# Graph layers on one core: products with adj as seven block products over pairs of batches, and one PSUM pool of eight banks

## The chip, the core and the metric

The kernel runs on one core of a Trainium2 chip. The metric is the device time of one execution in microseconds (us). The kernel before was run three times: median 1768.22 us, 1768.13 to 1768.93. One further execution was taken with the hardware profiler: 1770.05 us, of which 1768.3 us lie between its first and last instruction (the span).

Engines are named as in the profile: PE is the matrix engine (TensorE), PEld its weight loads, DVE the vector engine, ACT the scalar engine, POOL GpSimd, SP the engine that issues most transfers. PSUM is the memory that matmuls write to; the kernel uses it as eight banks of 128 x 512 f32 each. DVE and ACT read and write it.

## What is computed

x has 32 batches of 512 nodes by 128 channels, adj is 512 x 512, all in f32. Layer 0 is a graph convolution with three powers of adj, layer 1 five steps of a gated recurrent unit whose inputs are products with adj. Both get a residual and a layer norm. Cut to what matters:

```python
# layer 0: both "adjacencies" are adj, so the weights of equal powers add up
p1 = adj @ x; p2 = adj @ p1; p3 = adj @ p2
y  = x @ W[0] + p1 @ (W[1] + W[4]) + p2 @ (W[2] + W[5]) + p3 @ (W[3] + W[6])
h0 = layernorm(x + y)
# layer 1: 5 times, from h = h0; av = [m, m]
m  = adj @ h
u  = h @ u3.T + u3_b
z  = sigmoid([m, m] @ w3.T + w3_b + u)
r  = sigmoid([m, m] @ w4.T + w4_b + u)
hv = tanh([m, m] @ w5.T + w5_b + (r * h) @ u5.T + u5_b)
h  = (1 - z) * h + z * hv
out = layernorm(h0 + h)
```

## The kernel before

The host lays out adj transposed (adjT). The 32 batches go in eight groups of four (GB = 4). A batch is held twice: as nodes by channels, four tiles of 128 x 128 (xg, h0, h), and transposed, 128 channels by 512 nodes (xT, hT). The halves of w3, w4 and w5 are added once at the start (L103 to L108), so that one 128 x 128 weight serves.

**Layer 0** (L156 to L222) takes for each batch four transposes (ptr_x, L142), the product with adj (pt, L166: four matmuls of 512 columns, summed in one bank), a copy by ACT (tT), and eight matmuls of 128 columns into pq (L180, L181), which DVE copies to U. For the four batches together py (L190 to L202) applies adj squared (at2, made once) to U and adds the rest. ACT copies it to v, DVE takes moments, POOL the power -0.5 (rstd, L127), DVE normalises to h0 (L136), and four transposes per batch give the first hT.

**Layer 1** (L224 to L276) runs over five steps and in each over the group's four batches. I call one batch in one step a batch-step; there are 8 x 5 x 4 = 160. On PE it is:

- the product with adj: pm, four matmuls of 512 columns (L233), copied by ACT to mT (L237);
- pu (L239), then pr (L244), pz (L251) and w5, the first matmul into ph (L257), one matmul each;
- u5, the second matmul into ph (L258), which needs rh. rh comes from pr by a DVE addition (L245), ACT's sigmoid (L246) and a DVE product (L248). DVE's addition for pz (L252) stands between;
- four transposes into ptr_h (L142), which need the new hT. It comes from ph by ACT's tanh (L259) and three DVE operations (L261, L262, L264). ACT copies them back to h (L270), the operand of the next step's pm.

In the last step DVE adds h0 instead (L272) and last_norm follows (L145 to L154): moments, rstd on POOL, four normalisations (y), and a store by SP.

**What sets the order.** Each engine executes its own queue in order. The framework's scheduler makes the queues from the written order, the dependencies and its own model of time. It also hands out the buffers of the pools: here four pools of two PSUM banks (ps_mm, ps_zr, ps_hv, ps_tr). Layer 0 of the next group is a generator. After each batch-step but the group's first, the main loop (L282 to L288) lets it write one further piece, so that layer 0 of group g + 1 is written in between layer 1 of group g. On PE's queue of the old program the order is not the written one: the product of the next batch is placed between w5 and u5 of this one, and between u5 and the transposes.

Of the kernel before, what the change touches and what calls it, by code (L numbers as in the profile page):

```python
# [8 lines left out]
F32 = mybir.dt.float32  # L9
AF = mybir.ActivationFunctionType  # L10
ALU = mybir.AluOpType
PSUM = bass.MemoryType.PSUM

P = 128
NK = 4
# [7 lines left out]
def gnn_resnorm_kernel(  # L23
# [24 lines left out]
    small = ctx.enter_context(tc.tile_pool(name="small", bufs=4))  # L48
    ps_mm = ctx.enter_context(tc.tile_pool(name="ps_mm", bufs=2, space=PSUM))
    ps_zr = ctx.enter_context(tc.tile_pool(name="ps_zr", bufs=2, space=PSUM))  # L50
    ps_hv = ctx.enter_context(tc.tile_pool(name="ps_hv", bufs=2, space=PSUM))
    ps_tr = ctx.enter_context(tc.tile_pool(name="ps_tr", bufs=2, space=PSUM))

    def load_x(g):
        xg = grp.tile([P, NK, GB, P], F32, tag="xg", name=f"xg_{g}")
        for b in range(GB):
            nc.sync.dma_start(
                xg[:, :, b, :], x[g * GB + b].rearrange("(p k) c -> p k c", k=NK)
            )
        return xg  # L60
# [21 lines left out]

    an = const.tile([P, NK, N], F32, tag="an", name="an")
    at2 = const.tile([P, NK, N], F32, tag="at2", name="at2")
    for km in range(NK):
        ptr = ps_tr.tile([P, NK, P], F32, tag="tr", name=f"ptr_a_{km}")
        for k in range(NK):
            nc.tensor.transpose(ptr[:, k, :], at[:, k, km * P : (km + 1) * P], ident)
        nc.scalar.copy(an[:, km, :], ptr.rearrange("p k c -> p (k c)"))
    for k in range(NK):  # L90
        pq = ps_mm.tile([P, N], F32, tag="mm", name=f"pq_{k}")
        for km in range(NK):
            nc.tensor.matmul(  # L93
                pq,
                lhsT=an[:, km, k * P : (k + 1) * P],
                rhs=at[:, km, :],
                start=(km == 0),
                stop=(km == NK - 1),
            )
        nc.vector.tensor_copy(at2[:, k, :], pq)  # L100


# [35 lines left out]
    def transposed(src_of, name):  # L138

        ptr = ps_tr.tile([P, NK, P], F32, tag="tr", name=f"ptr_{name}")  # L140
        for k in range(NK):
            nc.tensor.transpose(ptr[:, k, :], src_of(k), ident)  # L142
        return ptr

    def last_norm(g, b, h):  # L145
# [10 lines left out]
    def layer0(g, xg, done):  # L156

        xTs, tTs = [], []
        U = grp.tile([P, NK, GB, P], F32, tag="U", name=f"U_{g}")
        for b in range(GB):  # L160
            ptr = transposed(lambda k: xg[:, k, b, :], f"x_{g}_{b}")
            xT = work.tile([P, NK, P], F32, tag="xT", name=f"xT_{g}_{b}", bufs=5)
            nc.scalar.copy(xT, ptr)
            pt = ps_mm.tile([P, NK, P], F32, tag="mm", name=f"pt_{g}_{b}")
            for k in range(NK):
                nc.tensor.matmul(  # L166
                    pt.rearrange("p k n -> p (k n)"),
                    lhsT=xg[:, k, b, :],
                    rhs=at[:, k, :],
                    start=(k == 0),  # L170
                    stop=(k == NK - 1),
                )
            tT = work.tile([P, NK, P], F32, tag="tT", name=f"tT_{g}_{b}", bufs=5)
            nc.scalar.copy(tT, pt)
            xTs.append(xT)
            tTs.append(tT)
            yield
            pq = ps_mm.tile([P, NK, P], F32, tag="mm", name=f"pq_{g}_{b}")
            for k in range(NK):
                nc.tensor.matmul(pq[:, k, :], lhsT=xT[:, k, :], rhs=wc[:, 2, :], start=True, stop=False)  # L180
                nc.tensor.matmul(pq[:, k, :], lhsT=tT[:, k, :], rhs=wc[:, 3, :], start=False, stop=True)  # L181
            nc.vector.tensor_copy(U[:, :, b, :], pq)  # L182
            yield

        v = grp.tile([P, NK, GB * P], F32, tag="v", name=f"v_{g}")
        mv = small.tile([P, NK * GB, 2], F32, tag="mv0", name=f"mv0_{g}")
        for ko in range(NK):
            py = ps_mm.tile([P, GB * P], F32, tag="mm", name=f"py_{g}_{ko}")
            for k in range(NK):
                nc.tensor.matmul(  # L190
                    py,
                    lhsT=at2[:, k, ko * P : (ko + 1) * P],
                    rhs=U[:, k, :, :].rearrange("p b o -> p (b o)"),
                    start=(k == 0),
                    stop=False,
                )
            for b in range(GB):
                dst = py[:, b * P : (b + 1) * P]
                nc.tensor.matmul(dst, lhsT=xTs[b][:, ko, :], rhs=wc[:, 0, :], start=False, stop=False)  # L199
                nc.tensor.matmul(  # L200
                    dst, lhsT=tTs[b][:, ko, :], rhs=wc[:, 1, :], start=False, stop=(b == GB - 1)
                )  # L202
            nc.scalar.copy(v[:, ko, :], py)
            for b in range(GB):
                moments(mv[:, ko * GB + b, :], v[:, ko, b * P : (b + 1) * P], f"{g}_{ko}_{b}")
            yield

        h0 = grp.tile([P, NK, GB, P], F32, tag="h0", name=f"h0_{g}")
        rstd = rstd_of(mv, NK * GB, f"0_{g}")
        hT = []  # L210
        for b in range(GB):
            for k in range(NK):
                i = k * GB + b
                normalise(
                    h0[:, k, b, :], v[:, k, b * P : (b + 1) * P], mv[:, i, 0:1], rstd[:, i : i + 1]
                )
            ptr = transposed(lambda k: h0[:, k, b, :], f"h0_{g}_{b}")
            t = work.tile([P, NK * P], F32, tag="hT0", name=f"hT_{g}_{b}_init", bufs=6)
            nc.scalar.copy(t, ptr.rearrange("p k c -> p (k c)"))
            hT.append(t)  # L220
            yield
        done.append((h0, hT))  # L222

    def layer1(g, h0, hT):  # L224


        h = [h0[:, :, b, :] for b in range(GB)]
        for s in range(STEPS):
            for b in range(GB):
                nm = f"{g}_{s}_{b}"  # L230
                pm = ps_mm.tile([P, N], F32, tag="mm", name=f"pm_{nm}")
                for k in range(NK):
                    nc.tensor.matmul(  # L233
                        pm, lhsT=h[b][:, k, :], rhs=at[:, k, :], start=(k == 0), stop=(k == NK - 1)
                    )
                mT = work.tile([P, N], F32, tag="mT", name=f"mT_{nm}")
                nc.scalar.copy(mT, pm)  # L237
                pu = ps_mm.tile([P, N], F32, tag="mm", name=f"pu_{nm}")
                nc.tensor.matmul(pu, lhsT=u3s, rhs=hT[b], start=True, stop=True)  # L239
                uT = work.tile([P, N], F32, tag="uT", name=f"uT_{nm}")  # L240
                nc.scalar.activation(uT, pu, AF.Identity, bias=ub3s)  # L241

                pr = ps_zr.tile([P, N], F32, tag="zr", name=f"pr_{nm}")
                nc.tensor.matmul(pr, lhsT=w4s, rhs=mT, start=True, stop=True)  # L244
                nc.vector.scalar_tensor_tensor(pr, pr, b4s, uT, ALU.add, ALU.add)  # L245
                nc.scalar.activation(pr, pr, AF.Sigmoid)  # L246
                rh = work.tile([P, N], F32, tag="rh", name=f"rh_{nm}")
                nc.vector.tensor_tensor(rh, pr, hT[b], ALU.mult)  # L248

                pz = ps_zr.tile([P, N], F32, tag="zr", name=f"pz_{nm}")  # L250
                nc.tensor.matmul(pz, lhsT=w3s, rhs=mT, start=True, stop=True)  # L251
# [3 lines left out]

                ph = ps_hv.tile([P, N], F32, tag="hv", name=f"ph_{nm}")
                nc.tensor.matmul(ph, lhsT=w5s, rhs=mT, start=True, stop=False)  # L257
# [4 lines left out]
                nc.vector.tensor_tensor(ph, ph, z, ALU.mult)  # L262
                hT_new = work.tile([P, NK * P], F32, tag="hT", name=f"hT_{nm}", bufs=8)
                nc.vector.tensor_tensor(hT_new, ph, hT[b], ALU.add)  # L264
                hT[b] = hT_new

                ptr = transposed(lambda k: hT_new[:, k * P : (k + 1) * P], f"h_{nm}")
                h_new = work.tile([P, NK, P], F32, tag="h", name=f"h_{nm}", bufs=6)
                if s < STEPS - 1:
                    nc.scalar.copy(h_new, ptr)  # L270
                else:
                    nc.vector.tensor_tensor(h_new, ptr, h0[:, :, b, :], ALU.add)  # L272
                h[b] = h_new
                if s == STEPS - 1:
                    last_norm(g, b, h_new)
                yield  # L276
# [5 lines left out]
    for g in range(NG):  # L282
        ahead = layer0(g + 1, load_x(g + 1), done) if g + 1 < NG else iter(())
        for i, _ in enumerate(layer1(g, *done[g])):
            if i >= 1:
                next(ahead, None)
# [55 lines left out]
```

## Time and profile before

| | |
|---|---|
| median of three runs | 1768.22 us (1768.13 to 1768.93) |
| the profiled execution | 1770.05 us |
| its span | 1768.3 us, 14169 instructions |
| mean granted clock of PE | 0.991 |
| a group's share, from 488 to 700 us | 212 us, PE busy 209.59, DVE 104.70, ACT 77.77, POOL 6.92 |
| read from and written to memory | 10.42 and 8.39 MB |
| a 512-column f32 matmul | two records of 592 ns, each at least 0.43 us after the one before |
| a load of x for one batch | 256 KB, 4.4 us to landing |

A matmul in f32 shows as two records with a weight load each, a transpose as one. Records of matmuls overlap: the next starts while one drains, so spacing and duration differ. Busy time counts overlapping records once. "Idle" in brackets is the time in which the engine did nothing ahead of an instruction, with what it waited for. The granted clock is the share of PE's full clock that the hardware allowed in a stretch.

### The profile page before, as it was taken

Reading aid. Unit: us, or ns where it says so; the run is one execution under the profiler, and the core shown is the slowest. Engines: PE = TensorE matmul, PEld = TensorE weight load, DVE = VectorE, ACT = ScalarE, POOL = GpSimd, SP = SyncE. Lnnn points to the kernel's source line nnn. Section 1 sums busy time; section 2 is a strip of 40 time slices with the busy share of each in tenths; the row PEclk is TensorE's granted clock in tenths of the full one; section 3 lists DMA queues with packets and bytes.
Section 4 is the critical chain, followed back from the end, with each engine's and each line's share of the span. In section 5 each row is a group of like instructions: output and inputs, shape, how many; then the busy total and the mean of one; then the engine's idle time right before and its main releaser. Section 6 shows DMA issues by size and latency. Waiting matters only on the chain.

```text
span 1768.3 us, 14169 instructions
## 1 busy us (share of the span) xinstructions
PE 1717.5 (97%) x5360; PEld 845.7 (48%) x5360; DVE 856.6 (48%) x1845; ACT 640.6 (36%) x1062; POOL 56.1 (3%) x46
## 2 busy tenths in 40 slices
PE   6899999999999999999999999999999999999997
PEld 3545544455445554455544555445544455444443
DVE  1244347444574445744356444564445543466556
ACT  1143334333433333333343332433324333344442
POOL 0000000000000000000000000000000000000000
PEclk9999999999999999999999999999999999999998
DMA  3000000000000000000000000000000000000000
GB/s 94 24 1 0 24 1 18 6 24 0 1 24 0 24 1 0 24 0 24 1 0 24 0 24 1 6 19 0 0 1 12 12 0 1 1 13 12 1 0 24
DMA packets 23684, 19.72 MB, mean 11 GB/s; under 512 B 1856, under 2 KB 19264, under 8 KB 23488
## 3 DMA queue, kind: packets, MB, share of 16 engines
q1 hardware_dynamic: 21504, 16.78, 3.0%
q10 hardware_dynamic: 2112, 2.03, 0.4%
q8 instruction: 42, 0.69, 0.2%
q14 instruction: 26, 0.21, 0.0%
HBM read 10.42 MB, written 8.39 MB: 11 GB/s over the span
## 4 chain that ended last, share of the span: by engine, by line
PE 93%; DVE 4%; POOL 1%; DMA 1%; issue 0%; ACT 0%; POOLq 0%; SPq 0%; DVEq 0%
PE pm L233 29%; PE ph L258 8%; PE pr L244 8%; PE pz L251 7%; PE pu L239 7%; PE ph L257 7%; PE py L190 6%; PE pt L166 6%; PE ptr_h L142 5%; PE pq L181 2%; PE py L200 2%; PE py L199 2%; PE pq L180 2%; POOL rstd L127 1%; DVE h L136 1%; PE pq L93 1%
## 5 line engine op out<-in xcount | busy, mean ns | idle before, releaser
L233 PE MATMUL pm<-at,h 128*128 128x512 f32 x1280 | 599.8, 598 | 0.0
L233 PEld LDWEIGHTS pm<-at,h 128*128 128x128 f32 x1280 | 239.6, 193 | 269.0 <-issue 269.0
L245 DVE SCALAR_TENSOR_TENSOR pr<-pr,b4s,uT 128x512 f32<-128x512 f32 x160 | 121.2, 757 | 418.7 <-PE pr L244 410.5
L237 ACT COPY mT<-pm 128x512 f32<-128x512 f32 x160 | 93.6, 585 | 353.8 <-PE pm L233 353.8
L261 DVE TENSOR_TENSOR ph<-ph,hT 128x512 f32<-128x512 f32 x128 | 89.4, 699 | 205.7 <-ACT ph L259 205.7
L259 ACT ACTIVATE ph<-ph,hv_b 128x512 f32<-128x512 f32 x160 | 105.9, 662 | 220.4 <-PE ph L258 220.4
L258 PE MATMUL ph<-rh,u5s 128*128 128x512 f32 x320 | 170.1, 614 | 16.1 <-DVE rh L248 16.1
L244 PE MATMUL pr<-mT,w4s 128*128 128x512 f32 x320 | 171.4, 617 | 0.0
L251 PE MATMUL pz<-mT,w3s 128*128 128x512 f32 x320 | 163.5, 592 | 0.0
L257 PE MATMUL ph<-mT,w5s 128*128 128x512 f32 x320 | 163.4, 592 | 0.0
L246 ACT ACTIVATE pr<-pr 128x512 f32<-128x512 f32 x160 | 93.4, 584 | 180.8 <-DVE pr L245 180.7
L239 PE MATMUL pu<-hT,u3s 128*128 128x512 f32 x256 | 130.8, 592 | 0.0
L252 DVE SCALAR_TENSOR_TENSOR pz<-pz,b3s,uT 128x512 f32<-128x512 f32 x160 | 121.0, 757 | 17.0 <-PE pz L251 13.5
L241 ACT ACTIVATE uT<-pu,ub3s 128x512 f32<-128x512 f32 x160 | 109.9, 687 | 42.4 <-PE pu L239 42.4
L190 PE MATMUL py<-U,at 128*128 128x512 f32 x256 | 119.7, 592 | 0.8 <-DVE U L182 0.8
L166 PE MATMUL pt<-at,xg 128*128 128x512 f32 x256 | 119.7, 592 | 0.0
L270 ACT COPY h<-ptr_h 128x512 f32<-128x512 f32 x128 | 74.9, 585 | 116.1 <-PE ptr_h L142 116.1
L142 PEld LDWEIGHTS ptr_h<-ident,hT 128*128 128x128 f32 x640 | 77.4, 141 | 82.2 <-issue 39.0
L254 ACT ACTIVATE z<-pz 128x512 f32<-128x512 f32 x160 | 95.5, 597 | 53.1 <-DVE pz L252 51.9
L262 DVE TENSOR_TENSOR ph<-ph,z 128x512 f32<-128x512 f32 x160 | 111.6, 698 | 4.5
L127 POOL TENSOR_TENSOR rstd<-ve,mhalf 128x4 f32<-128x4 f32 (+1 forms) x40 | 55.4, 1385 | 1707.3 <-DVE ve L125 1707.3
L142 PE MATMUL ptr_h<-ident,hT 128*128 128x128 f32 x640 | 97.1, 274 | 6.2 <-DVE hT L264 4.1
(59 smaller groups left out, 1420.7 us busy)
## 6 DMA issues: line engine op xcount, KB each, us to landing
xg<-in_x SPq DMA_DIRECT2D x32, 256.0 KB, 4.4
out<-y SPq DMA_DIRECT2D x32, 256.0 KB, 2.0
at<-in_adjT ACTq DMA_DIRECT2D x1, 1024.0 KB, 6.5
w_raw<-in_w ACTq DMA_DIRECT2D x1, 448.0 KB, 3.2
w3s_raw<-in_w ACTq DMA_DIRECT2D x1, 128.0 KB, 6.0
w4s_raw<-in_w ACTq DMA_DIRECT2D x1, 128.0 KB, 5.4
w5s_raw<-in_w ACTq DMA_DIRECT2D x1, 128.0 KB, 5.4
u3s<-in_u ACTq DMA_DIRECT2D x1, 64.0 KB, 4.6
```

The source lines that it names most:

```text
L142: nc.tensor.transpose(ptr[:, k, :], src_of(k), ident)
L166: nc.tensor.matmul(pt.rearrange("p k n -> p (k n)"), lhsT=xg[:, k, b, :], rhs=at[:, k, :], start=(k == 0), stop=(k == NK - 1),)
L190: nc.tensor.matmul(py, lhsT=at2[:, k, ko * P : (ko + 1) * P], rhs=U[:, k, :, :].rearrange("p b o -> p (b o)"), start=(k == 0), stop=False,)
L233: nc.tensor.matmul(pm, lhsT=h[b][:, k, :], rhs=at[:, k, :], start=(k == 0), stop=(k == NK - 1))
L239: nc.tensor.matmul(pu, lhsT=u3s, rhs=hT[b], start=True, stop=True)
L244: nc.tensor.matmul(pr, lhsT=w4s, rhs=mT, start=True, stop=True)
L245: nc.vector.scalar_tensor_tensor(pr, pr, b4s, uT, ALU.add, ALU.add)
L251: nc.tensor.matmul(pz, lhsT=w3s, rhs=mT, start=True, stop=True)
L252: nc.vector.scalar_tensor_tensor(pz, pz, b3s, uT, ALU.add, ALU.add)
L257: nc.tensor.matmul(ph, lhsT=w5s, rhs=mT, start=True, stop=False)
L258: nc.tensor.matmul(ph, lhsT=u5s, rhs=rh, start=False, stop=True)
L262: nc.vector.tensor_tensor(ph, ph, z, ALU.mult)
```

## The change

Three things change.

**Products with adj over pairs of batches.** With node blocks of 256 and two batches side by side, the operand and adj's transpose are each 2 x 2 blocks, and their product needs eight block products the plain way. The new `adj_product` takes seven (Winograd's form). Four sums T of adj's blocks are made once by DVE (new L109 to L113). Four sums S of the batches' blocks are made each time by POOL, 128 x 256 each (L162 to L165). Each block product is two matmuls of 256 columns. Three banks collect them: pb one product; pc two; pa four one after another, and ACT copies pa out after each, three times to Q and at last to m1, while the sum goes on. DVE adds pb and pc to copies in Q (three additions). The results m0 and m1 take the place of tT in layer 0 and mT in layer 1, for two batches.

```diff
+    def adj_product(X, name):
+        X11, X12, X21, X22 = X[:, 0, :H], X[:, 0, H:], X[:, 1, :H], X[:, 1, H:]
+        S = work.tile([P, 4, H, P], F32, tag="S", name=f"S_{name}", bufs=3)
+        nc.gpsimd.tensor_tensor(S[:, 0], X21, X22, ALU.add)
+        nc.gpsimd.tensor_tensor(S[:, 1], S[:, 0], X11, ALU.subtract)
+        nc.gpsimd.tensor_tensor(S[:, 2], X11, X21, ALU.subtract)
+        nc.gpsimd.tensor_tensor(S[:, 3], X12, S[:, 1], ALU.subtract)
...
+        pa, pb, pc = (bank(f"p{i}_{name}")[:, :HN] for i in "abc")
...
+        product(pa, X11, B11, True, False)
+        nc.scalar.copy(Q[:, 0], pa)
+        product(pb, X12, B21, True, True)
+        product(pa, S[:, 1], T[:, 1], False, False)
+        nc.vector.tensor_tensor(m0[:, :HN], pb, Q[:, 0], ALU.add)
+        nc.scalar.copy(Q[:, 1], pa)
+        product(pc, S[:, 0], T[:, 0], True, False)
+        product(pa, S[:, 2], T[:, 2], False, False)
+        nc.scalar.copy(Q[:, 2], pa)
+        nc.vector.tensor_tensor(m1[:, HN:], pc, Q[:, 2], ALU.add)
+        product(pa, X22, T[:, 3], False, True)
+        nc.scalar.copy(m1[:, :HN], pa)
+        product(pc, S[:, 3], B22, False, True)
+        nc.vector.tensor_tensor(m0[:, HN:], pc, Q[:, 1], ALU.add)
+        return m0, m1
```

**One PSUM pool.** Every PSUM tile is now one of eight banks of a single pool.

```diff
-    ps_mm = ctx.enter_context(tc.tile_pool(name="ps_mm", bufs=2, space=PSUM))
-    ps_zr = ctx.enter_context(tc.tile_pool(name="ps_zr", bufs=2, space=PSUM))
-    ps_hv = ctx.enter_context(tc.tile_pool(name="ps_hv", bufs=2, space=PSUM))
-    ps_tr = ctx.enter_context(tc.tile_pool(name="ps_tr", bufs=2, space=PSUM))
+    psum = ctx.enter_context(tc.tile_pool(name="psum", bufs=8, space=PSUM))
+
+    def bank(name):
+        return psum.tile([P, N], F32, tag="bank", name=name)
```

**Where the pieces are cut.** The product is written ahead of each pair's first batch, with a yield behind it, in both layers. Layer 0's transposes of x come behind the product. The main loop lets layer 0 go on after every second piece of layer 1, and after all of them from the 21st on.

```diff
-                pm = ps_mm.tile([P, N], F32, tag="mm", name=f"pm_{nm}")
-                for k in range(NK):
-                    nc.tensor.matmul(
-                        pm, lhsT=h[b][:, k, :], rhs=at[:, k, :], start=(k == 0), stop=(k == NK - 1)
-                    )
-                mT = work.tile([P, N], F32, tag="mT", name=f"mT_{nm}")
-                nc.scalar.copy(mT, pm)
+                if b % 2 == 0:
+                    m = adj_product(h[b // 2], f"h_{nm}")
+                    if s < STEPS - 1:
+                        h[b // 2] = work.tile([P, 2, NK, P], F32, tag="h", name=f"h_{nm}", bufs=4)
+                    yield
+                mT = m[b % 2]
...
         for i, _ in enumerate(layer1(g, *done[g])):
-            if i >= 1:
+            if i % 2 == 1 or i > 20:
                 next(ahead, None)
```

Besides, xg and h0 are stored batch by batch, h holds two batches per tile, U has one buffer instead of two, and some buffer counts change (uT and rh 3, h 4, mT 6).

## The prediction

> **What bounds the kernel now.** The first view is the page's busy times, with the shares of the chain that ended last:
>
> ```profile
> PE 1717.5 (97%) x5360; PEld 845.7 (48%) x5360; DVE 856.6 (48%) x1845; ACT 640.6 (36%) x1062; POOL 56.1 (3%) x46
> ...
> PE 93%; DVE 4%; POOL 1%; DMA 1%; issue 0%; ACT 0%; POOLq 0%; SPq 0%; DVEq 0%
> ```
>
> TensorE (PE) is full: it idles 1768.3 - 1717.5 = 51 us in all, two thirds of that before the loop and in its last 20 us. So both the matmul work and anything that opens a hole in PE's in-order queue count in full. How it is kept full is seen in the timeline of one batch-step (start, duration, engine, line):
>
> ```profile
> 700.18 1.02 PE L244 MATMUL pr<-mT,w4s 128*128 128x512 f32 x2
> 701.04 1.02 PE L251 MATMUL pz<-mT,w3s 128*128 128x512 f32 x2
> 701.31 0.76 DVE L245 SCALAR_TENSOR_TENSOR pr<-pr,b4s,uT 128x512 f32<-128x512 f32 x1 [2.38 <-PE pr L244]
> 701.90 1.02 PE L257 MATMUL ph<-mT,w5s 128*128 128x512 f32 x2
> ...
> 702.10 0.58 ACT L246 ACTIVATE pr<-pr 128x512 f32<-128x512 f32 x1 [0.95 <-DVE pr L245]
> ...
> 702.76 1.02 PE L233 MATMUL pm<-at,h 128*128 128x512 f32 x2
> ...
> 702.77 0.68 DVE L248 TENSOR_TENSOR rh<-pr,hT 128x512 f32<-128x512 f32 x1
> ...
> 703.61 1.02 PE L258 MATMUL ph<-rh,u5s 128*128 128x512 f32 x2
> ...
> 704.47 2.74 PE L233 MATMUL pm<-at,h 128*128 128x512 f32 x6
> ...
> 704.67 0.66 ACT L259 ACTIVATE ph<-ph,hv_b 128x512 f32<-128x512 f32 x1 [1.19 <-PE ph L258]
> ...
> 705.37 0.70 DVE L261 TENSOR_TENSOR ph<-ph,hT 128x512 f32<-128x512 f32 x1 [1.92 <-ACT ph L259]
> ...
> 706.10 0.70 DVE L262 TENSOR_TENSOR ph<-ph,z 128x512 f32<-128x512 f32 x1
> ...
> 706.83 0.69 DVE L264 TENSOR_TENSOR hT<-ph,hT 128x512 f32<-128x512 f32 x1
> ...
> 707.05 1.02 PE L239 MATMUL pu<-hT,u3s 128*128 128x512 f32 x2
> ...
> 707.91 0.60 PE L142 MATMUL ptr_h<-ident,hT 128*128 128x128 f32 x4
> ```
>
> Two chains leave PE and come back. From pr (700.18) through DVE, ACT and DVE, rh is ready at 702.77 + 0.68 = 703.45, and 0.06 later (as where PE really waits, below) u5, the second matmul into ph, could start: 3.33 after pr. From u5 (703.61) through tanh and three DVE operations hT is ready at 707.52; with the 0.15 between hT and the transposes seen at the end of the trace they could start 4.06 after u5. PE fills both times with the next batch's product with adj: one matmul of pm before u5, three and pu after it. In the order of the old program's instructions at least 0.86 us of such other work stands before u5 in 159 of the 160 batch-steps, and at least 3.43 us between u5 and the transposes, also in 159. The last batch has no other work, and there the trace shows the bare price (idle time in brackets; its 3.63 has 0.6 of DVE's y in it):
>
> ```profile
> 1759.55 1.09 PE L142 MATMUL ptr_h<-ident,hT 128*128 128x128 f32 x4 [3.63 <-DVE hT L264]
> ```
>
> Third, what a hole does to the clock. Stretches of 3.41 us: PE busy is the second number, the granted clock (PEclk) the one before the DMA share:
>
> ```profile
> 461.80:465.20 3.40, 1.62 (x4) 0.87 (x5) 2.23 (x6) 1.64 (x3) 0.00 (x0) 1.00 0.00 0
> 465.20:468.60 3.40, 3.40 (x12) 1.55 (x11) 2.36 (x4) 1.48 (x3) 0.00 (x0) 1.00 0.00 0
> ```
> ```profile
> 673.41:676.82 3.41, 1.33 (x5) 0.27 (x3) 3.41 (x10) 1.18 (x2) 0.00 (x0) 1.00 0.00 0
> 676.82:680.23 3.41, 3.41 (x4) 1.48 (x5) 1.06 (x3) 0.66 (x1) 0.00 (x0) 0.50 0.03 5
> ```
>
> Once per group u5 waits 2.08 us. In five groups of seven the idle time lies in one clock window, which is 39% busy, and the next window runs at 0.50; in the other two (47% here) nothing happens. In all of them pm stands ready behind u5 and isn't run first: PE does not pass a waiting matmul.
>
> **The matmul work.** A 512-column f32 matmul is two records, 0.43 us start to start, 0.86 together; a 128-column one takes 0.223 (layer 0: six in 1.34). On that line 256 columns cost 0.435 (between half of 0.86 and twice 0.223). A pair of batches had 8 x 0.86 = 6.88; it gets 14 x 0.435 = 6.09. There are 80 pairs in layer 1 and 16 in layer 0: 96 x 0.79 = **-76 us**.
>
> **The lost cover.** This is what decides. In the order of the new program pr, pz, w5, u5 and the four transposes stand directly one after another in all 160 batch-steps. The products and layer 0's pieces come behind the transposes, or ahead of pr. So u5 waits 3.33 - 3 x 0.86 = 0.75 us, and the transposes 4.06 - 0.86 = 3.20, with the next pu or product queued behind them. For 159 batch-steps: 119 + 509 = **+628 us**.
>
> **Waits inside the product.** In 45 of 80 pairs pr follows the last product directly and waits for m0: matmul drain 0.16 (a record of 592 ns at a spacing of 429), 0.11 to DVE, its 256-column add, 0.06 back. An add of 256 isn't in the trace: between 0.29 (128 columns, L107) and 0.70 (512, L261); on the line between, 0.43. That is 0.76 x 45 = +34 (28 to 46). The third use of pa waits for ACT's copy of 256 columns, between 0.29 (half of 0.585) and 0.585; I take the middle, 0.44. It is hidden by 0.87 of other products or pu, except in 30 pairs where only four transposes (0.44) stand between: 0.26 x 30 = +8 (3 to 12). In 14 pieces of layer 0 xT's copy stands behind h's on ACT, and the transposes cover 0.87 of 1.9: +14. Each new semaphore wait on PE may hold back the weight load ahead, between 0 and 0.08 (pr to pz is 0.94 instead of 0.86 where pr has just waited): about 5 in each of 96 products, middle 0.04, +19 (0 to 38). In return the old 0.08 at pr goes, -13. The normalisation of h0 still stands in DVE's queue ahead of a chain once per group, now with two more operations inside it: +4.
>
> **What costs nothing.** The copies and adds are 4 x 0.44 on ACT and 3 x 0.43 on DVE per pair, less two copies of 0.585; with PE at over 25 us per pair neither is near full. If they were late, they would be late at the waits priced above. POOL's four sums work on h finished a pair earlier, over 15 us. No 256-column sum is in the trace: a 128-column select on POOL took 0.29; rstd's power, 16 columns, 2.90, which at that rate would be 46 us. By kind an add is nearest to the select; 0.6 to 1.2 each, 5 us a pair at most. Only from about 4 us each does PE wait. rstd now stands behind up to four sums; its readers (y) are off the path. The x loads land in 4.4 us, a group ahead.
>
> **The clock.** Holes of about 3.0 us (3.20 less the drain), after one of 0.6, come 160 times. Halving takes 1.8 to 2.1 us idle in a 3.41 us window; with 1.95 the window may start anywhere in 3.15 us around the hole: 92%. The half-speed window then begins 1.35 to 4.5 us after the hole's start; on average 2.96 us of it lie behind the hole and cost half, 1.48: 160 x 0.92 x 1.48 = 218. If a half-speed window that is partly idle doesn't release the clock, about 290; some falls on pz and w5, which have room. I take **+240** (100 to 400). The 8.5 of the old five windows go.
>
> The Trainium skill, "TensorE: Matmul & The Clock Gate" (Part 1: The HAM clock gate), has the clock fall only after a whole idle window of about 3.4 us. By it these holes would cost no clock and the sum would be 2380. The 39% window above says otherwise, and I follow it.
>
> **Sum**, against the profiled execution: 1768.3 - 76 + 628 + 34 + 8 + 14 + 19 - 13 + 4 - 8 + 240 = 2618; with 1.75 around the span, as there (1770.05), **2620 us**. The shown median, 1768.22, is 0.1% below the profiled run, far less than any term.
>
> **Rivals.**
> - The waits come, the clock stays up: 2620 - 240 = 2380. For it: two of seven holes didn't drop it. Against: 3 us is half as long again. 0.10.
> - Faster: PE does not stand at the transposes, since the queued product runs past the waiting matmul, and the two chains stay covered as now. Then only the -76 and the small waits (34 + 8 + 14 + 19 - 13 + 4 = 66) are left: 1760; without those, 1694. It decides once 618 of the 628 us are covered. Against it: u5's 2.08 us with pm ready behind. 0.03.
> - A new engine bounds: POOL's sums, above 4 us each. At 8 us a pair takes 32 us, 96 pairs 3070 us. For it only the power's rate. 0.03.
> - The clock hardly recovers, since each half-speed window holds the next hole: two windows per hole, 160 x 2 x 1.7 = 544, 2920. Against: a fully busy window releases it, and between holes lie 5 to 12 us of work. 0.06.
>
> The forecast's own case, clock cost 100 to 400, has 0.78. The range 2400 to 2800 reaches to the first rival's edge and takes in the other bounds (together about 60 us either way). Slower by over 0.2% (about what a measurement of this kernel can tell from no change): 0.965; within it 0.005; faster 0.03.
>
> **What would show it.** PE's busy share near 72% (68 to 76); PE's waits led by the transposes for hT, about 500 us in 160 times, then u5 for rh, about 120; 256-column records 0.217 apart; mean granted clock about 0.90 instead of 0.99 (160 x 0.92 windows of 3.41 us at half); POOL's sums under 1.2 us. Wrong it would be if the transposes' wait is under 1 us each, if the clock stays at 0.99 (2380), or if the 256-column records are bound by their 0.19 us weight loads plus a wait each and come 0.3 apart (+220).

## The result and the profile after

The changed kernel takes 2688.76 us (median of four runs, 2688.23 to 2689.09), the kernel before took 1768.58 us beside it. The ratio is 1.52, with a 95% interval of 1.517 to 1.523: half as long again. The forecast was 2620 us.

The busy times and the shares of the chain that ended last, of the changed kernel:

```profile
PE 2028.6 (75%) x6512; PEld 1249.5 (46%) x6512; DVE 997.5 (37%) x2137; ACT 683.1 (25%) x1254; POOL 326.4 (12%) x430
...
PE 69%; DVE 23%; ACT 4%; issue 2%; POOL 1%; DMA 0%; ACTq 0%; POOLq 0%; DVEq 0%
```

Two things are to be seen. PE is no longer full: it idles 2687.3 - 2028.6 = 659 us instead of 51, and DVE's share of the chain has gone from 4% to 23%. And PE is busy 311 us longer than before, although the products got smaller. Busy time that grows while the work shrinks is for the most part work done at a lower clock. (A smaller part is how it is counted: the last 0.16 us of a matmul, which the next one used to cover, now count by themselves ahead of each of the 365 waits in the first three lines below, some 58 us.)

PE's waits name the idle time (line waited for: us in total, times, longest):

```profile
PE ptr_h L155 <- DVE hT L309: 502.6, 160, 5.1
PE ph L303 <- DVE rh L293: 95.0, 160, 0.9
PE pr L289 <- DVE m_h L196: 23.2, 45, 0.5
PE pq L225 <- ACT xT L220: 10.8, 16, 0.7
```

The first two lines hold 598 of the 659 us, once in each of the 160 batch-steps. No line names POOL. The timeline of one batch-step shows them in place:

```profile
1004.93 1.02 PE L289 MATMUL pr<-m_h,w4s 128*128 128x512 f32 x2
1005.79 1.02 PE L296 MATMUL pz<-m_h,w3s 128*128 128x512 f32 x2
1006.65 1.02 PE L302 MATMUL ph<-m_h,w5s 128*128 128x512 f32 x2
...
1007.52 0.68 DVE L293 TENSOR_TENSOR rh<-pr,hT 128x512 f32<-128x512 f32 x1
1008.25 1.13 PE L303 MATMUL ph<-rh,u5s 128*128 128x512 f32 x2 [0.58 <-DVE rh L293]
...
1011.64 0.69 DVE L309 TENSOR_TENSOR hT<-ph,hT 128x512 f32<-128x512 f32 x1
1012.38 1.12 PE L155 MATMUL ptr_h<-ident,hT 128*128 128x128 f32 x4 [3.00 <-DVE hT L309]
...
1014.14 1.84 PE L284 MATMUL pu<-hT,u3s 128*128 128x512 f32 x2
```

u5 starts 3.32 us after pr and the transposes 4.13 us after u5, as long as the chains through DVE and ACT take; nothing lies inside but this batch's own pz and w5. And the pu behind them takes 1.84 us instead of 1.02. The stretches of 3.41 us around it say why (PE busy is the second number, the granted clock the one before the DMA share):

```profile
1005.53:1008.95 3.42, 2.84 (x7) 0.89 (x6) 2.11 (x3) 1.47 (x3) 0.00 (x0) 1.00 0.00 0
1008.95:1012.36 3.41, 0.43 (x1) 0.00 (x0) 2.09 (x3) 0.66 (x1) 0.00 (x0) 1.00 0.00 0
1012.36:1015.78 3.42, 3.40 (x10) 2.44 (x11) 0.00 (x0) 1.17 (x2) 0.00 (x0) 0.50 0.02 5
...
1036.26:1039.67 3.41, 1.13 (x2) 0.30 (x2) 1.40 (x3) 0.87 (x2) 0.00 (x0) 1.00 0.00 0
1039.67:1043.08 3.41, 2.47 (x6) 1.59 (x7) 2.13 (x7) 0.00 (x0) 0.00 (x0) 0.50 0.00 0
1043.08:1046.50 3.42, 3.42 (x5) 1.35 (x4) 1.33 (x6) 1.15 (x2) 0.00 (x0) 0.50 0.00 0
1046.50:1049.91 3.41, 2.22 (x5) 0.49 (x3) 2.53 (x7) 1.16 (x3) 1.02 (x1) 1.00 0.00 0
```

A stretch that is 13% busy (0.43 of 3.41) is followed by one at 0.50, and that one, full, by one at 1.00. The second hole costs two: the half-speed stretch itself is only 72% busy (2.47), and the next one is still at 0.50. A stretch at full speed that is 65% busy (2.22) has done no harm. Over the whole trace the clock falls 162 times and lies at half for 774 us, which is 227 such stretches. PE is busy for 657 us of them; half of that, 329 us, is time that full speed would have saved, if half the clock makes all of it twice as long.

### The profile page after: what moved, and what is told of

The parts are those of the page before. It is cut to its first block, busy times and chain, and to the rows that moved or that the text cites. A ratio compares the mean times of both kernels' runs of the same rounds, so it can differ in the third digit from the quotient of the medians.

```text
span 2687.3 us, 17885 instructions
## 1 busy us (share of the span) xinstructions
PE 2028.6 (75%) x6512; PEld 1249.5 (46%) x6512; DVE 997.5 (37%) x2137; ACT 683.1 (25%) x1254; POOL 326.4 (12%) x430
## 4 chain that ended last, share of the span: by engine, by line
PE 69%; DVE 23%; ACT 4%; issue 2%; POOL 1%; DMA 0%; ACTq 0%; POOLq 0%; DVEq 0%
PE pa_h L174 13%; PE pu L284 6%; PE ph L303 6%; PE pr L289 6%; PE ptr_h L155 6%; PE py L236 6%; PE pc_h L174 5%; PE pz L296 5%; DVE ph L307 4%; DVE ph L306 4%; DVE hT L309 4%; DVE pz L297 4%; ACT ph L304 4%; PE pb_h L174 4%; DVE rh L293 4%; PE pa_x L174 3%
## 5 line engine op out<-in xcount | busy, mean ns | idle before, releaser
L155 PE MATMUL ptr_h<-ident,hT 128*128 128x128 f32 x640 | 153.7, 386 | 502.6 <-DVE hT L309 502.6
L162 POOL TENSOR_TENSOR S_h<-h 128x256 f32<-128x256 f32 x80 | 57.8, 723 | 1725.5 <-ACT h L314 1699.9
L289 PE MATMUL pr<-m_h,w4s 128*128 128x512 f32 x320 | 199.5, 710 | 23.2 <-DVE m_h L196 23.2
L296 PE MATMUL pz<-m_h,w3s 128*128 128x512 f32 x320 | 176.9, 636 | 0.0
L174 PE MATMUL pa_h<-T,S_h 128*128 128x256 f32 x640 | 169.3, 388 | 0.0
L302 PE MATMUL ph<-m_h,w5s 128*128 128x512 f32 x320 | 163.4, 592 | 0.0
L303 PEld LDWEIGHTS ph<-rh,u5s 128*128 128x128 f32 x320 | 47.6, 188 | 227.5 <-DVE rh L293 227.5
L174 PE MATMUL pa_h<-at,h 128*128 128x256 f32 x320 | 142.0, 594 | 0.0
L174 PEld LDWEIGHTS pa_h<-T,S_h 128*128 128x128 f32 x640 | 127.4, 199 | 20.8
L289 PEld LDWEIGHTS pr<-m_h,w4s 128*128 128x128 f32 x320 | 71.2, 234 | 118.8 <-issue 69.9
```

The lines of the kernel that those rows point to most:

```text
L155: nc.tensor.transpose(ptr[:, k * P : (k + 1) * P], src_of(k), ident)
L174: nc.tensor.matmul(dst, lhsT=left[:, k, :], rhs=right[:, k, :], start=(first and k == 0), stop=(last and k == H - 1), skip_group_check=True,)
L303: nc.tensor.matmul(ph, lhsT=u5s, rhs=rh, start=False, stop=True)
```

## Experiments

The theory that the experiments test has two parts. One ring of eight banks for all PSUM tiles makes the scheduler keep the written order, so that nothing stands between a batch's own matmuls; and the holes that this opens halve the clock. The rivals: the seven-product form itself (POOL's sums, more waits, shorter matmuls) brings the loss; or the clock is of no account, and the idle time and some other delay explain it all. Each run is given with the kernel before beside it; ratios have a 95% interval.

### One ring of banks in the kernel before

```diff
-    ps_mm = ctx.enter_context(tc.tile_pool(name="ps_mm", bufs=2, space=PSUM))
-    ps_zr = ctx.enter_context(tc.tile_pool(name="ps_zr", bufs=2, space=PSUM))
-    ps_hv = ctx.enter_context(tc.tile_pool(name="ps_hv", bufs=2, space=PSUM))
-    ps_tr = ctx.enter_context(tc.tile_pool(name="ps_tr", bufs=2, space=PSUM))
+    psum = ctx.enter_context(tc.tile_pool(name="psum", bufs=8, space=PSUM))
+    ps_mm = ps_zr = ps_hv = ps_tr = psum     # and tag="bank" on every PSUM tile
```

> The kernel before with its four PSUM pools of two banks made one pool of eight, and nothing else: eight-matmul products, old order of writing. Theory (the single pool fixes the order: a tile gets its bank only after every tile written before it, so no later product can be put between w5, u5 and the transposes): in the built order pr, pz, w5, u5 and the transposes stand directly one after another in all 160 batch-steps, so u5 waits 0.75 us and the transposes 3.2 us each, 628 us in all, and the clock falls as in the changed kernel (about 330 us there): about 2700 us, within 60 of the changed kernel. Rival (the seven-product form, its sums, copies and added waits cost the time): about 1770.

Measured: 2735.72 us, ratio 1.546 (1.544 to 1.549), clock 0.853. The products with adj are the old ones. In the trace's order pr, pz, w5, u5 and the transposes stand directly one after another in all 160 batch-steps, as in the changed kernel, and PE's waits are nearly the same:

```profile
PE ptr_h L140 <- DVE hT L262: 476.9, 160, 3.1
PE ph L256 <- DVE rh L246: 116.1, 160, 3.8
```

So the ring alone makes the whole loss, and a little more than the whole change does.

### Eight rings of one bank in the changed kernel

A tag names a ring of buffers inside a pool. Here seven kinds of tiles get a ring of one bank each, and all others share the eighth.

```diff
-    psum = ctx.enter_context(tc.tile_pool(name="psum", bufs=8, space=PSUM))
+    psum = ctx.enter_context(tc.tile_pool(name="psum", bufs=1, space=PSUM))
+    TAGS = {"pa": "pa", "pb": "pb", "pc": "pc", "pr": "r", "pz": "z", "ph": "hv", "ptr": "tr"}
...
-        return psum.tile([P, N], F32, tag="bank", name=name)
+        return psum.tile([P, N], F32, tag=TAGS.get(name.split("_")[0], "mm"), name=name)
```

> The changed kernel with the one PSUM tag of eight banks divided into eight tags of one bank each: pa, pb, pc, pr, pz, ph, the transposes, and one for the rest. Seven-product form and order of writing stay. Theory (pool): later products come between the chains again (0.86 us or more ahead of u5 in 159 of 160, 3.9 us or more between u5 and the transposes in 157), so the 628 us and the clock's part go and the 76 us of saved matmul work remain, less the product's own waits of 20 to 70: 1710 to 1770 us. Rival (the seven-product form costs): above 2500.

Measured: 1719.49 us (1718.79 to 1720.20), ratio 0.972 (0.9705 to 0.9736). It beats both kernels. The first two lines are its busy times and chain, the next its longest waits, and the last its PE timeline around one batch-step:

```profile
PE 1651.4 (96%) x6512; PEld 1050.1 (61%) x6512; DVE 952.0 (55%) x2137; ACT 665.1 (39%) x1254; POOL 326.1 (19%) x430
...
PE 86%; DVE 9%; POOL 3%; issue 1%; ACT 1%; DMA 0%; SPq 0%; ACTq 0%; POOLq 0%; DVEq 0%
```
```profile
PE ph L304 <- DVE rh L294: 20.7, 14, 2.5
PE ptr_h L156 <- DVE hT L310: 9.6, 8, 4.9
```
```profile
1042.33 1.02 PE L290 MATMUL pr<-m_h,w4s 128*128 128x512 f32 x2
1043.18 1.02 PE L297 MATMUL pz<-m_h,w3s 128*128 128x512 f32 x2
1044.04 2.74 PE L237 MATMUL py<-U,at 128*128 128x512 f32 x6
1046.62 0.60 PE L156 MATMUL ptr_h<-ident,hT 128*128 128x128 f32 x4
1047.06 1.02 PE L303 MATMUL ph<-m_h,w5s 128*128 128x512 f32 x2
1047.91 1.02 PE L304 MATMUL ph<-rh,u5s 128*128 128x512 f32 x2
1048.77 1.02 PE L237 MATMUL py<-U,at 128*128 128x512 f32 x2
...
1051.42 0.60 PE L175 MATMUL pa_h<-at,h 128*128 128x256 f32 x2
1051.97 0.63 PE L156 MATMUL ptr_h<-ident,hT 128*128 128x128 f32 x4
```

Layer 0's py and the next pair's product stand again between pr and u5 and between u5 and the transposes, which come 4.06 us after u5 with no idle time before them. All parts of the change but the ring are still there. It is therefore not "one pool" that costs, since this is also one pool, but one ring in which each tile takes the next bank. In the three traces with the ring and without useless matmuls (the changed kernel, the kernel before with the ring and the one with eight products below) u5 and the transposes follow each other directly in all 160 batch-steps; with the tags something stands between them in 159. Why the scheduler keeps the written order with such a ring no run shows.

### Holes filled with work of no use

Matmuls whose result nobody reads go into a bank of their own, right behind u5, in the changed kernel; the ring has the other seven banks. Nothing else is altered.

```diff
+                fill = junk.tile([P, N], F32, tag="fill", name=f"fill_{nm}")
+                for _ in range(3):          # 2 and 1 in two further kernels
+                    nc.tensor.matmul(fill, lhsT=ident, rhs=rh, start=True, stop=True)
```

> The changed kernel with three dummy 512-column matmuls behind u5 in each batch-step, reading rh and writing a bank of their own that nothing reads (seven banks are left for the rest). 413 us of matmul work more. Theory (the holes halve the clock, and that is about 330 us of the time): they run in the 3.0 us hole, leave it at about 0.5, the clock stays up and the time falls by 250 to 340: about 2360 us, mean granted clock above 0.97. Rival (the clock's part is small, or follows the kernel and not the holes): 2690, or up to 3100 if the dummies delay the chain.

> The same with two matmuls without use. About 1.3 us of idle time is left ahead of the transposes, so that every window is at least 60% busy. Theory: no drops, the waits of the transposes absorb the one matmul less, 2370 to 2385 us, clock above 0.98. Rival (it is the number of holes, not their length): 2690 us, 0.86.

> The changed kernel (one PSUM pool) with one matmul of 512 columns without use behind u5, into a bank of its own, instead of three. About 2.1 us of idle time is left ahead of the transposes. Theory (a window of 3.41 us that is less than about half busy drops the clock): the clock still drops for some two thirds of the holes, whose idle time lies in one window for 1.7 us or more: 2374 + 105 x about 2 us, 2500 to 2650 us, clock 0.87 to 0.95. Rival (any hole on this place drops the clock): 2690 us, 0.856. Rival (the idle time must be longer than 2.1 us): 2375 us, 0.99.

The wait view's line for the transposes, for three, two and one matmuls, each from its own kernel:

```profile
PE ptr_h L156 <- DVE hT L313: 84.1, 160, 2.5
```
```profile
PE ptr_h L156 <- DVE hT L313: 221.3, 160, 3.3
```
```profile
PE ptr_h L156 <- DVE hT L313: 358.6, 160, 4.2
```

| matmuls in each hole | idle ahead of the transposes, mean | falls of the clock | granted clock | median time, ratio |
|---|---|---|---|---|
| none (the changed kernel) | 3.14 us | 162 | 0.856 | 2688.76 us, 1.520 (1.517 to 1.523) |
| one | 2.24 us | 89 | 0.932 | 2525.03 us, 1.428 (1.426 to 1.431) |
| two | 1.38 us | 14 | 0.988 | 2385.95 us, 1.349 (1.347 to 1.351) |
| three | 0.53 us | 5 | 0.995 | 2374.13 us, 1.342 (1.340 to 1.345) |

With one I had expected some 105 falls, and 89 came; with two none, and 14 came. With three, PE has 160 x 3 x 0.86 = 413 us more to do, the idle time falls by 502.6 - 84.1 = 418 us, so these cancel, and the kernel is 315 us faster. The order and both chains are the same; the ring has one bank less. That is the clock's part by itself, beside the 329 us worked out from the records. The second rival, that the clock is of no account, falls. So does the rule that only a hole's presence matters: with two matmuls every step still has one of 1.38 us, and the clock falls 14 times instead of 162.

### Seven products against eight

In both kernels below the pair's product is written the plain way, without S and Q, once with the ring of eight banks and once with tags (seven of them: two batches' products, pr, pz, ph and the transposes with one bank each, and two banks for the rest, since pc is free). So the second kernel differs from the one with seven products and eight tags not in the product alone, as its expectation says, but also in that bank.

```diff
-        product(pa, X11, B11, True, False)
-        nc.scalar.copy(Q[:, 0], pa)
...
+        for i in range(2):
+            pm = bank(f"pm{i}_{name}")
+            for k in range(NK):
+                nc.tensor.matmul(pm, lhsT=X[:, i, k, :], rhs=at[:, k, :], start=(k == 0), stop=(k == NK - 1))
+            mT = work.tile([P, N], F32, tag="mT", name=f"m{i}_{name}", bufs=6)
+            nc.scalar.copy(mT, pm)
```

> The changed kernel with the plain product in adj_product: for each of the two batches four 512-column matmuls and one copy, no sums on POOL, no Q; one pool and order of writing stay. Theory: the order of pr, pz, w5, u5, transposes is unchanged, so the holes and the clock stay; 76 us more of matmul work, some of it at half clock, against 30 to 70 us of waits in the product that go: 2690 to 2750. Rival (the seven-product form costs the time): 1770 to 1900.

> The product with adj the plain way, eight block products (four matmuls of 512 columns per batch, one ACT copy each; no S, Q, pa, pb, pc), in the changed kernel with eight tags of one PSUM bank. It differs from the kernel with seven products and eight tags in the product alone. Theory (with the chains covered, PE is full and the seven products are worth their matmul time): 96 pairs x 0.79 us more matmul, less the product's small waits of a few us, so 1719 + 50 to 76 = 1770 to 1795 us, PE busy about 96%, clock above 0.98. Rival (the division of the banks, not the product, made the kernel with eight tags faster than the one before): about 1719 us, within 10.

With the ring: 2739.72 us, ratio 1.549 (1.547 to 1.551), 51 us above seven products. Some 12 of them are a wait for xT, 22.4 us here where seven products have 10.8:

```profile
PE pq L199 <- ACT xT L194: 22.4, 32, 0.7
```

With the tags: 1758.54 us, ratio 0.994 (0.993 to 0.996), 39 us above seven products, below the expected 1770 to 1795 us. The seven products are a gain in both, so the first rival falls; they are worth some 39 us, half of what their matmuls alone would give. Where the other half is, the busy times of the second kernel show:

```profile
PE 1703.0 (97%) x5360; PEld 841.0 (48%) x5360; DVE 848.0 (48%) x1849; ACT 644.3 (37%) x1062; POOL 56.2 (3%) x46
```

Its PE is busy 1703.0 - 1651.4 = 51.6 us longer, not 76. Added up from the records of both traces, from each start to the next and without idle time, the products take 667 us here and 596 with seven: 70 us, so nearly all of the 76 arrives. Some 19 us go back in the other matmuls, 7 of them in pu. PE also idles 54 us in this kernel's span of 1757.2 us where seven products idle 66: u5's 20.7 us stand only with seven, while the transposes wait 9.6 us with seven and 29.5 us here. These waits can't be put down to the product alone, since the banks differ too.

### POOL's sums done twice

In the kernel with eight tags, whose PE is full, the four sums S are written a second time. Is their hiding deep, or only just enough?

```diff
+        for _ in range(2):
             nc.gpsimd.tensor_tensor(S[:, 0], X21, X22, ALU.add)
             nc.gpsimd.tensor_tensor(S[:, 1], S[:, 0], X11, ALU.subtract)
             nc.gpsimd.tensor_tensor(S[:, 2], X11, X21, ALU.subtract)
             nc.gpsimd.tensor_tensor(S[:, 3], X12, S[:, 1], ALU.subtract)
```

> The kernel with seven products and eight tags, with POOL's four sums S per product done twice, the second time into the same places. POOL's work per pair goes from 2.9 to 5.8 us. Theory (the sums lie a pair earlier than their readers and are hidden): within 5 us of 1719 us, and no wait of PE for POOL. Rival (POOL's sums hold back PE, or share memory ports with DVE so that its operations get longer): 96 x 2.9 us = up to 279 us more, about 2000 us; half covered, 1860 us.

Measured: 1802.87 us, ratio 1.018 (1.016 to 1.021): 83 us more. My expectation of 5 us failed, and so did the size of the rival's. PE idles 48 us longer than with single sums, and it is busy 36 us longer with the same work, since the clock falls 19 times instead of twice (0.976 for 0.996). Its longest waits:

```profile
PE ph L305 <- DVE rh L295: 33.5, 14, 3.3
PE pc_h L176 <- DVE m_h L194: 25.9, 7, 3.7
PE pa_h L176 <- POOL S_h L165: 11.3, 8, 2.8
```

Only the last, 11.3 us, names POOL, whose own line is unchanged (727 ns a sum in both). The second is new, and the first was 20.7 us with single sums. The cause of both stands on DVE. One place of seven like it, in the timeline:

```profile
1165.33 0.30 DVE L147 BATCH_NORM_AGGREGATE mv<-st 128x2 f32<-128x6 f32 x2
...
1165.67 3.57 DVE L139 TENSOR_SCALAR ve<-mv 128x4 f32<-128x4 f32 x1
1165.73 0.74 POOL L166 TENSOR_TENSOR S_x<-xg 128x256 f32<-128x256 f32 x1
1166.41 0.74 POOL L167 TENSOR_TENSOR S_x<-xg,S_x 128x256 f32<-128x256 f32 x1
...
1168.47 0.74 POOL L165 TENSOR_TENSOR S_x<-S_x,xg 128x256 f32<-128x256 f32 x1
1169.15 0.69 DVE L308 TENSOR_TENSOR ph<-ph,hT 128x512 f32<-128x512 f32 x1
1169.29 0.73 POOL L167 TENSOR_TENSOR S_x<-xg,S_x 128x256 f32<-128x256 f32 x1
1169.97 1.02 POOL L141 TENSOR_TENSOR rstd<-ve,mhalf 128x4 f32<-128x4 f32 x1
1171.03 0.35 DVE L150 TENSOR_SCALAR y<-hf,mv,rstd 128x128 f32<-128x128 f32 x1 [1.19 <-POOL rstd L141]
```

ve, sixteen bytes a partition, takes 3.57 us instead of 0.17. It ends in the first gap between POOL's sums (1169.21 to 1169.29); while they follow each other without one it doesn't end. In all seven places it takes 3.56 to 3.58 us and outlasts five sums. The moments beside the same kind of sums (1165.33) take their usual time, and the operations that read PSUM have the same means as with single sums, within 5 ns (m_h 421, ph 698). Behind ve stand the tanh chain's operations and an m_h in DVE's queue, and rstd, for which y waits, stands behind the sums in POOL's. The product that adds on to the bank that this m_h reads starts at 1173.22, after 3.73 us of idle time on PE, one of the seven waits for m_h above.

The Trainium skill, "SBUF — State Buffer" (SBUF: two separate sides), has a pair of SBUF ports shared by DVE and GpSimd, held as an exclusive lock for a whole instruction by whichever starts first, a GpSimd operation or a DVE operation that is in a two-port mode or has two SBUF inputs. A ve that doesn't end beside a sum fits that, but here it waited through five, and whether it runs in such a mode, and that it is this lock, was not tested.

Two further kernels double only half of the products each, to see whether the cost is that of the place or of each sum:

```diff
+        inner = name[0] == "h" and name.split("_")[2] in "123"
+        for _ in range(2 if inner else 1):      # 1 if inner else 2 in the other kernel
```

> As with the doubled sums (seven products, eight tags), but POOL's sums are done twice only for the products of steps 1 to 3 of layer 1 (counted from 0), 48 of the 96 products. The doubling of all cost 83 us. Theory: that cost arises only where a series of sums meets the norms or the h0 just made, which is at step 0, at layer 0's products and in the last step (there DVE's ve is held up to 3.6 us while POOL's sums run without a gap, rstd stands behind the sums, and the h0 of step 0 is summed directly ahead of its product): within 6 us of 1719 us, ve's mean near 0.2 us. Rival (each second set of sums costs the same everywhere, 83/96 = 0.87 us, by a load on memory or on DVE): 1719 + 42 = 1761 us.

> The complement: the sums are done twice for layer 0's 16 products and for those of steps 0 and 4, 48 of the 96. Theory: nearly all of the 83 us, 1790 to 1805 us, with ve held as in the doubling of all. Rival (the same cost everywhere): 1761 us.

Measured: steps 1 to 3 doubled 1735.95 us, ratio 0.982 (0.980 to 0.983), 16.5 us more; the others doubled 1786.20 us, ratio 1.009 (1.008 to 1.011), 66.7 us more. Together 83.2 us, as the doubling of all. The cost is mainly that of the place, but not only: I expected at most 6 and at least 71 us. In the first, ve's longest is 0.43 us, and a wait is left that I hadn't counted:

```profile
PE pa_h L177 <- POOL S_h L166: 8.7, 8, 1.2
```

Once in a group a product follows so soon on its h that even the inner sums are late when doubled, by 1.2 us in seven of the groups; PE's time at half clock also goes up by some 20 us, which takes about 10 more. In the second, ve reaches 3.55 us, y waits 44.3 us for rstd instead of 23.1, and PE's queue shows nearly the same waits as with all sums doubled (those that name POOL are 2.7 us instead of 11.3). So the single sums are hidden in the kernel with eight tags, but at one place of each group not deeply: in its trace the sum that a product waits for ends 1.54 us ahead of it there, in seven groups of eight.

## Why the prediction was right

The mechanism held at each step that decides; the distance of 68 us (2.6%) lies in the clock, with small terms against it.

- **The lost cover** was right in place, and nearly in size. Idle time of 0.59 and 3.14 us a batch-step was measured where the forecast, less the drain of 0.16 us, has 0.59 and 3.04. 153 waits of the transposes lie at 3.00 to 3.10 us; seven, one in a group, take 5.04 to 5.08, where the normalisation of h0 stands between the operations of the tanh chain in DVE's queue. They make most of the excess, 14 us. But in the kernel before u5 waited 2.08 us for this normalisation in seven places, 14.6 us that are in its 1768.3: it only moved, and the forecast's +4 for it did not come. (The "about 120 us" for u5 in the list of signs had the drain still in it; 95.0 is the same wait.) The runs add what I had only read from the order: the ring makes it, with or without seven products.
- **The clock** is the step that failed in size: "+240 (100 to 400)" measured 315 to 329 us. The number of falls was nearly right (160 x 0.92 = 147; 162 came, at most two of them ahead of the loop). What failed is "on average 2.96 us of it lie behind the hole and cost half, 1.48": I let each fall last one stretch. It lasted 227 / 162 = 1.4, because a half-speed stretch that is itself partly idle often doesn't release the clock, the case I priced at about 290 and set aside. In the first stretches behind the falls PE is busy for 443 us, which costs 222 where the forecast has 218; the 65 later ones cost the other 107 us. For the same reason the mean clock was 0.856, not about 0.90.
- **The skill's rule**, "TensorE: Matmul & The Clock Gate" (Part 1: The HAM clock gate), that a whole idle window is needed, would have given 2380. The trace disagrees: the windows 13% and 33% busy were enough, and filling the holes gave back 315 us.
- **The matmul work** was right: four 256-column records in 0.86 to 0.87 us, 0.216 apart. Its -76 us don't arrive in full: net of their waits, seven products are worth 51 us in this kernel, 39 without xT's part (and 39 with PE full), where the forecast's terms net to -76 + 34 + 8 + 19 - 13 = -28.
- **The waits inside the product** were a little too large. m0's is 23.2 us of idle time, 0.52 us each and 0.68 with the drain, for 0.76: the add took 0.424 us as I had it on the line between, so the rest came sooner. The copies of 256 columns took 0.372, not 0.44 us, and no wait for Q or pa is left: 0 for +8. xT's is 10.8 for +14. The +19 for held-back weight loads can't be told apart here; with PE full, the 19 us that went back in the matmuls beside the products are what it could look like.
- **POOL's sums** took 0.72 us, inside 0.6 to 1.2, and no matmul waits for them in the changed kernel. But "only from about 4 us each does PE wait" is wrong for a full PE: doubling them, as if each took 1.45 us, cost 83 us with eight tags. In the changed kernel it was not tested.

With what was measured, the clock 75 to 89 us more, 3 + 8 + 3 less for m0, Q and xT, and 4 + 0.6 less for h0's normalisation, the sum is 2618 + 75 - 19 = 2674 at the least and 2688 at the most, against a span of 2687.3. The 39 us of the seven products agree with it: the forecast's 28, and 11 from m0 and Q. That no larger term is left over does not show that each small one is right.

Of the rivals, the first came nearest in kind: the kernel with three matmuls in each hole is "the waits come, the clock stays up", and it takes 2374 us where 2380 was worked out. The second, covered chains, is the kernel with eight tags: 1719 us, inside 1694 to 1760, though by the order of PE's queue and not, as that rival had it, by PE passing a waiting matmul.

## What to carry to other kernels

How PSUM banks are divided into rings is part of the order of work: here, with rings by kind of tile, a later batch's work passed a waiting stage, and with one common ring it never did. So read the order on the full engine before and after such a change, and price each chain that leaves the engine against the work that stands inside it. And where a hole of some 3 us can't be covered, it cost twice here: the idle time, and half of what ran in the stretches behind it; one of 1.4 us cost little beside its idle time (14 falls).

## What was not expected of the hardware

- Adding 413 us of matmuls without use made the kernel 315 us faster (2689 to 2374 us), since it kept the clock up.
- Falling and rising have different bounds, counted over the whole traces. In the changed kernel all stretches at full clock up to 47% busy were followed by half speed and none from 57% on; in the other runs both are seen between 41% and 48%, so busy time alone doesn't decide there. At half speed no stretch below 79% busy was followed by full speed in any run and all from 86% on were; between, both are seen (2.75 of 3.42 us, 80%, at 1022.60 released it).
- A DVE operation of 0.17 us was held for 3.57 us while POOL's sums of 0.73 us followed each other without a gap.
